# Rows fetched by register on two queues in layers 2 and 3 of a graph network, and the K and V products in halves of the array

## The chip, the cores and the metric

The kernel runs on one core of a Trainium2 chip. The metric is the time of one execution on the device in microseconds. Five engines work side by side on a core: TensorE (PE in the profile), VectorE (DVE), ScalarE (ACT), GpSimd (POOL) and SyncE (SP). SP and ACT can issue transfers between the memory outside the core (DRAM below) and the tiles on the core; GpSimd issues the indirect transfers, which fetch or store one row per lane by a tile of row numbers.

## What is computed

Four layers of a graph network run over 12500 nodes with 64 features each and 400000 edges sorted by destination. After every layer the result is added to the features and normalized:

```python
x = layernorm(x + L0(x))   # max over a node's edges of relu([x_i, x_j - x_i] @ W1 + b1) @ W2 + b2
x = layernorm(x + L1(x))   # edge features summed by source, then a two-layer product
x = layernorm(x + L2(x))   # mean over a node's edges of x[src], a gate of 3 groups, @ W_lin.T + b_lin
x = layernorm(x + L3(x))   # attention: 4 heads, 8 edge types, softmax over a node's edges

# layer 2, the part that matters here
msg_sum = segment_sum(x[src], dst)
# layer 3, the part that matters here
kw, m = typed_head_linear(k[src], rel_att, etype), typed_head_linear(v[src], rel_msg, etype)
a = (kw * qw).sum(-1) * rel_pri[:, etype].T / sqrt(16)
h = segment_sum(m * softmax_by_dst(a), dst)
```

## The kernel before

The edges are laid out as 128 lanes of 3125 edges. Column c of a lane is its c-th edge, and one column over all lanes is a "tile" of 128 edges. Columns are taken in groups of 25 (`G`); there are 124 whole groups, and the last 25 columns are split into groups of 16, 8 and 1 (`groups`). A helper, `gather` (L211), has GpSimd fetch one tile: 128 rows of a table in DRAM, by the 128 numbers in one column.

**The order of the stages.** First the edges are counted and the layer 1 edge features sorted. Then come: the edge stage of layers 0 and 1 (pools `e0`), which writes running results for every edge to the tables R0 and R1; the node stage of both (`n1`), which gathers each node's last row from R0 (tile `ga`) and R1 (tile `g1`), seven 128-node tiles at a time, and writes the features to the table X2; the edge stage of layer 2 (`e2`); its node stage (`n2`), which also makes the tables of layer 3; the edge stage of layer 3 (`e3`); and the last node stage (`n3`).

**Layer 2, edges.** For each group the rows of X2 are fetched into a tile `gx` of 25 columns. VectorE then adds column after column (L1127): what was summed so far, times a 0 or 1 that says whether the edge still belongs to the same node, plus the row. The group then goes to the table R2 in one store on ACT's queue (L1130). In every third group (`ROWS2 = 3`, 41 groups) the last column is not gathered by GpSimd. SP fetches it row by row instead: `row_by_row` loads 16 row numbers (`RL`) into registers (L1112) and issues 16 transfers of 256 bytes (L1117), eight times for a column. There are four `gx` buffers, and the order of the instructions is left to the planner.

**Layer 2, nodes.** For each batch of seven 128-node tiles, `nodes2` gathers the nodes' rows from R2, applies the gate and the product, normalizes, and makes K, V and Q. It then makes, for each of 8 edge types, a row of 128 numbers: 64 of K and 64 of V times that type's matrices. These rows form the table TKM. K lies in partitions 0 to 63 of `kv` and V in 64 to 127; the weights `wkm` hold both products with zeros in between, so that each product of TensorE (L1244) runs over all 128 partitions and yields four edge types. ScalarE moves the result out (L1246). `in_turn` sets the order of these stages by hand for all engines but GpSimd.

**Layer 3, edges.** For each group GpSimd gathers 25 columns of 512-byte rows of TKM into a tile `gk` (three buffers), and SP loads the query rows into `st` (L1273). VectorE carries the queries along the lane (L1278), multiplies and sums for the scores (L1285, L1286), and scans for the running maxima M (L1293). ScalarE takes the exponentials (`weight`, L1301, and `ex`, L1302) and spreads the decays (`dec`, L1308); VectorE forms `wm` (L1313) and runs the scan `hs` (L1318). ScalarE copies hs, M and L into the tile R (L1321 to L1323), and SP stores R to the table R3 (L1324). The planner orders all of it.

Of the kernel before, what the change touches and what calls it, by code (L numbers as in the profile page):

```python
# [9 lines left out]
F32 = mybir.dt.float32  # L10
# [31 lines left out]
WAIT2 = 16  # L42
WAIT3, EVERY3 = 2, 1
ACTN = 3
ROWS2 = 3
RL = 16
ZC = 200


# [1 line left out]
def resnorm_gnn_kernel(ctx: ExitStack, tc: tile.TileContext, a: dict, out: bass.AP):  # L51
# [158 lines left out]
    def gather(to, table, at):  # L210
        return nc.gpsimd.indirect_dma_start(  # L211
            out=to, out_offset=None, in_=table, in_offset=bass.IndirectOffsetOnAxis(ap=at, axis=0)
        )

    def same_keys(psp, sb, key, n, each=None, want_count=False):

# [188 lines left out]
    wkm = const.tile([P, ETY, 2, D], F32, name="wkm")  # L405
    nc.vector.memset(wkm, 0.0)
    for h in range(NH):
        nc.sync.dma_start(
            wkm[D + h * HS : D + (h + 1) * HS, :, 1, h * HS : (h + 1) * HS],
            a["L3_gnn_rel_msg"][h].rearrange("t d o -> d t o"),  # L410
        )

# [408 lines left out]
    with tc.tile_pool(name="ini", bufs=1) as ini, tc.tile_pool(name="inips", bufs=1, space=PSUM) as ips:  # L821
# [31 lines left out]
        for t in range(ETY):  # L853
            pr_ = ips.tile([P, 4, P], F32, name="ps_k")[:D, 0, :D]
            nc.tensor.transpose(pr_, ratt[:, t, :], ident[:D, :D])
            rT = ini.tile([D, D], F32, name="rT", bufs=2)
            nc.vector.tensor_copy(rT, pr_)
            pg = ips.tile([P, 4, P], F32, name="ps_k")[:D, 0, :D]
            nc.tensor.matmul(pg, rT, rT, start=True, stop=True)
            nc.vector.tensor_scalar(wkm[:D, t, 0, :], pg, prib[:, t : t + 1], None, op0=ALU.mult)  # L860


        nothing = ini.tile([1, W3], F32, name="nothing")
# [47 lines left out]
    def ends_of_lanes(sb, table, W, fixG=fixG):  # L911

        row = sb.tile([P, W], F32, name="row", bufs=1)
        gather(row, table[: E + 1, :], fixG)
        return row
# [4 lines left out]
        )  # L920

    to_l0.close()

    with (tc.tile_pool(name="e0", bufs=2) as sb, tc.tile_pool(name="e0ps", bufs=2, space=PSUM) as psp,
          tc.tile_pool(name="e0p1", bufs=1, space=PSUM) as ps1):
# [80 lines left out]
        for g, (c0, ng) in enumerate(groups):  # L1006
            gb = sb.tile([P, ng, D], F32, name="gb", bufs=3)
            if g in early:
                nc.sync.dma_start(gb, early_rows(early[g]))
            else:  # L1010
                for j in range(ng):
                    gather(gb[:, j, :], TB, srcS[:, c0 + j : c0 + j + 1])
            st = sb.tile([P, ng, D], F32, name="st", bufs=3)
            load = nc.sync.dma_start(st, lanes(S)[:, c0 : c0 + ng, :])
            for put in puts0:
                after(load, put, "reads what they write")
            for j in range(ng):
                c = c0 + j
                nc.vector.scalar_tensor_tensor(st[:, j, :], pa, keep[:, c : c + 1], st[:, j, :],  # L1019
                                               op0=ALU.mult, op1=ALU.add)  # L1020
                pa = st[:, j, :]
            R = sb.tile([P, ng, D], F32, name="R", bufs=2)
            for q in range(0, ng, 8):
                n = min(8, ng - q)
                msg = messages(gb, st, q, n, g in early)
                for j in range(q, q + n):
                    c = c0 + j
                    nc.vector.scalar_tensor_tensor(R[:, j, :], pm, negm[:, c : c + 1], msg[:, j - q, :],  # L1028
                                                   op0=ALU.add, op1=ALU.max)
                    pm = R[:, j, :]  # L1030
            nc.sync.dma_start(lanes(R0)[:, c0 : c0 + ng, :], R)
            while done < NG and done * R1G <= g * NG:
                key, pm1 = sums(done, key, pm1)
                done += 1
                if done == NG:
                    end_sums()
        row = ends_of_lanes(sb, R0, D)
        ps = carry_over(ps1, sb, pm)
        u = sb.tile([D, P], F32, name="u0", bufs=1)
        nc.vector.tensor_tensor_scan(u, neg64, ps, NEG, ALU.add, ALU.max)  # L1040
        nc.vector.tensor_max(row, row, shifted(ps1, sb, u, "g0"))
        put_ends(R0, row)


    with tc.tile_pool(name="n1", bufs=1) as sb, tc.tile_pool(name="n1ps", bufs=2, space=PSUM) as psp:
# [5 lines left out]
        def nodes01(b, t0, nt):  # L1051
# [8 lines left out]
            g1 = tile_of([P, nt, D + 1], "g1")  # L1060
            for j in range(nt):
                gather(g1[:, j, :], R1[: E + 1, :], lastE1[:, t0 + j : t0 + j + 1])
            comb = tile_of([P, nt, 2 * D], "comb", 8)
            for _ in range(WAIT1):
                yield
# [24 lines left out]
            nc.sync.dma_start(rows_of(X2, t0, nt), xb)  # L1090

        in_turn(nodes01, [NB] * (NBA - 1) + [4, 2, 1], lambda n: EVERY1)


    with tc.tile_pool(name="e2", bufs=2) as sb, tc.tile_pool(name="e2ps", bufs=1, space=PSUM) as psp:
        pm = sb.tile([P, D], F32, name="m2", bufs=1)
        nc.vector.memset(pm, 0.0)

        single = [g for g in range(2, NG - 1) if g % ROWS2 == 0]
        ns = len(single)  # L1100
        assert single == list(range(single[0], NG - 1, ROWS2)) and ns <= P
        at = groups[single[0]][0] + G - 1
        sf = sb.tile([P, ns], F32, name="sf", bufs=1)
        nc.vector.tensor_copy(sf, srcS[:, at : at + (ns - 1) * ROWS2 * G + 1 : ROWS2 * G])
        ps = psp.tile([P, P], F32, name="ps_i")
        nc.tensor.transpose(ps[:ns, :], sf, ident)
        numbers = sb.tile([P, P], I32, name="numbers", bufs=1)
        nc.vector.tensor_copy(numbers[:ns, :], ps[:ns, :])

        def row_by_row(to, k):  # L1110
            for p in range(0, P, RL):
                _, rows = nc.values_load_multi_w_load_instructions(  # L1112
                    numbers[k : k + 1, p : p + RL], engines=[mybir.EngineType.SP], min_val=0, max_val=NP - 1,
                    skip_runtime_bounds_check_because="src is the number of a node",
                )
                for r, row in enumerate(rows):
                    nc.sync.dma_start(to[p + r : p + r + 1, :], X2[ds(row, 1), :])  # L1117

        for g, (c0, ng) in enumerate(groups):
            gx = sb.tile([P, ng, D], F32, name="gx", bufs=4)  # L1120
            if g in single:
                row_by_row(gx[:, ng - 1, :], single.index(g))
            for j in range(ng - (g in single)):
                gather(gx[:, j, :], X2, srcS[:, c0 + j : c0 + j + 1])
            for j in range(ng):
                c = c0 + j
                nc.vector.scalar_tensor_tensor(gx[:, j, :], pm, keep[:, c : c + 1], gx[:, j, :],  # L1127
                                               op0=ALU.mult, op1=ALU.add)
                pm = gx[:, j, :]
            nc.scalar.dma_start(lanes(R2)[:, c0 : c0 + ng, :], gx)  # L1130
# [34 lines left out]
    with tc.tile_pool(name="n2", bufs=1) as sb, tc.tile_pool(name="n2ps", bufs=2, space=PSUM) as psp:  # L1165
        puts = []

        def nodes2(b, t0, nt):
# [65 lines left out]
            for j in range(nt):  # L1234
# [13 lines left out]
                nc.sync.dma_start(  # L1248
                    TKM[r * ETY : (r + P) * ETY, :].rearrange("(p e) f -> p (e f)", e=ETY),
                    km.rearrange("p w f -> p (w f)"),  # L1250
                )
                yield

# [4 lines left out]
    with tc.tile_pool(name="e3", bufs=2) as sb, tc.tile_pool(name="e3ps", bufs=1, space=PSUM) as psp:  # L1258
# [9 lines left out]
        for c0, ng in groups:  # L1268
            gk = sb.tile([P, ng, 2 * D], F32, name="gk", bufs=3)
            for j in range(ng):  # L1270
                gather(gk[:, j, :], TKM, stS[:, c0 + j : c0 + j + 1])
            st = sb.tile([P, ng, D], F32, name="st", bufs=2)
            load = nc.sync.dma_start(st, lanes(S)[:, c0 : c0 + ng, :])  # L1273
            for put in puts:
                after(load, put, "reads what they write")
            for j in range(ng):
                c = c0 + j
                nc.vector.scalar_tensor_tensor(st[:, j, :], pa, keep[:, c : c + 1], st[:, j, :],  # L1278
# [44 lines left out]
            nc.scalar.activation(R[:, :, D + NH :], L.rearrange("p h c -> p c h"), AF.Copy)  # L1323
# [117 lines left out]
```

## Time and profile before

| What | Value |
|---|---|
| Time, median of 3 runs | 16696.17 us (16695.95 to 16697.46) |
| Time of the profiled execution | 16699.22 us |
| Its span, first to last instruction | 16697.4 us |
| Busy: POOL, DVE, PE, ACT | 12548.5, 9601.6, 5362.8, 2673.4 us |
| Mean granted TensorE clock | 0.628 |
| Gathers of layer 2 (gx), of layer 3 (gk) | 3084, 3125 |
| Rows fetched by SP in layer 2 | 5248 |

A busy share is an average over stages that have different limits. In the list of groups a line gives the source line, the engine, the operation, what is written and read, the count, then busy time, mean length in nanoseconds and the idle time before these instructions with what ended it. "issue" is time in which the engine waited for nothing that the profile shows. SPq and ACTq are the instructions on those engines that issue transfers or work on registers; they are not counted as busy.

### The profile page before, as it was taken

How to read it: one execution, taken by the hardware profiler on the slowest of the kernel's cores; microseconds unless marked ns; L12 is line 12 of the kernel's file. 1: busy time of each engine (PE TensorE's matmuls, PEld its weight loads, DVE VectorE, ACT ScalarE, POOL GpSimd, SP SyncE). 2: the span in 40 equal slices, each digit the busy share in tenths (PEclk: the TensorE clock that was granted, in tenths of full speed). 3: DMA queues.
4: the chain of work that ended last, by engine and by line, in shares of the span. 5: the costliest groups of instructions: out<-in, count | busy, mean ns of one | idle time of the engine just before them, and what ended most of it. 6: DMA issues, size and time to landing. Idle time of an engine off the chain costs nothing. (4 is left out here: it accounts for less than half of the span.)

```text
span 16697.4 us, 162726 instructions
## 1 busy us (share of the span) xinstructions
PE 5362.8 (32%) x42392; PEld 4426.1 (27%) x42392; DVE 9601.6 (58%) x28242; ACT 2673.4 (16%) x4960; POOL 12548.5 (75%) x13066
## 2 busy tenths in 40 slices
PE   4445666666653666666400000000051000000002
PEld 4444555554542555555300000000030000000002
DVE  9996777777753777776322222222235565555556
ACT  0012333333321111111100000000022122122112
POOL 7777777777777777777777777777776777777776
PEclk6667777777766777777655555555575555555555
DMA  2333333222222555555211111111143333333333
GB/s 81 119 103 90 85 85 85 63 54 54 53 53 57 203 199 198 205 200 172 60 52 52 55 53 55 53 55 53 54 146 128 107 109 109 107 108 107 109 107 97
DMA packets 1116080, 1640.30 MB, mean 98 GB/s; under 512 B 740851, under 2 KB 741235, under 8 KB 1114755
## 3 DMA queue, kind: packets, MB, share of 16 engines
q1 hardware_dynamic: 653490, 987.85, 17.6%
q0 software_dynamic: 417824, 533.15, 12.2%
q10 hardware_dynamic: 43824, 108.83, 1.7%
q8 instruction: 337, 5.52, 0.1%
q14 instruction: 605, 4.95, 0.1%
HBM read 891.71 MB, written 737.15 MB: 98 GB/s over the span
## 5 line engine op out<-in xcount | busy, mean ns | idle before, releaser
L734 POOL DMA_INDIRECT SRT<-at,to x3125 | 3036.9, 972 | 952.5 <-issue 945.5
L211 POOL DMA_INDIRECT gk<-TKM,stS x3125 | 2975.6, 952 | 952.4 <-issue 926.8
L211 POOL DMA_INDIRECT gx<-X,srcS x3084 | 2921.0, 947 | 966.9 <-issue 907.5
L1127 DVE SCALAR_TENSOR_TENSOR gx<-gx,keep 128x64 f32<-128x64 f32 x3124 | 917.9, 294 | 2945.4 <-DMA gx<-X,srcS 1839.7
L211 POOL DMA_INDIRECT gb<-TB,srcS x2125 | 2076.0, 977 | 651.7 <-issue 625.2
L1028 DVE SCALAR_TENSOR_TENSOR R<-R,negm,msg 128x64 f32<-128x64 f32 x3124 | 854.0, 273 | 791.3 <-PE msg L959 786.9
L899 PE MATMUL ps_c<-ident,full 128*64 128x128 f32 x3 | 1.3, 421 | 3943.1 <-DVE full L1330 3942.0
L899 PE MATMUL ps_c<-ident,gx 128*64 128x128 f32 x1 | 0.4, 422 | 3867.6 <-DVE gx L1127 3867.6
L1285 DVE TENSOR_TENSOR pr<-st,gk 128x320 f32<-128x320 f32 x627 | 308.3, 492 | 1556.5 <-DMA gk<-TKM,stS 1551.5
L211 POOL DMA_INDIRECT xg<-in_x,srcS x1000 | 954.9, 955 | 306.0 <-issue 299.6
L899 PEld LDWEIGHTS ps_c<-ident,full 128*64 128x64 f32 x3 | 0.4, 129 | 3944.5 <-DVE full L1330 3942.8
L899 PEld LDWEIGHTS ps_c<-ident,gx 128*64 128x64 f32 x1 | 0.1, 129 | 3867.9 <-DVE gx L1127 3867.9
L337 DVE TENSOR_TENSOR ol<-iota,lo 128x512 f16<-128x512 f32 (+2 forms) x1000 | 979.1, 979 | 0.0
L1278 DVE SCALAR_TENSOR_TENSOR st<-st,keep 128x64 f32<-128x64 f32 x3124 | 868.4, 278 | 46.1
L953 PE MATMUL pt<-ident,st 128*128 128x128 f32 (+1 forms) x3250 | 825.9, 354 | 213.8 <-DVE st L1019 196.2
L1019 DVE SCALAR_TENSOR_TENSOR st<-st,keep 128x64 f32<-128x64 f32 x3124 | 863.7, 276 | 1.5
L694 PE MATMUL pG<-ol,mb 128*128 128x128 f16 x4625 | 778.0, 242 | 195.4 <-ACT mb L678 193.9
L987 DVE SCALAR_TENSOR_TENSOR r<-r,keep 128x64 f32<-128x64 f32 x3000 | 830.4, 277 | 0.1
L334 DVE TENSOR_TENSOR oh<-iota,hi 128x392 f16<-128x392 f32 (+2 forms) x1000 | 784.3, 784 | 24.0 <-DMA xg<-in_x,srcS 24.0
L646 PE MATMUL pT<-identh,oh 128*98 128x128 f16 x3125 | 413.3, 263 | 1180.3 <-DVE oh L334 1178.2
L952 PE MATMUL pt<-ident,gb 128*128 128x128 f32 (+1 forms) x2210 | 571.6, 353 | 565.6 <-DMA gb<-TB,srcS 561.3
L694 PE MATMUL pG<-A,hT 98*128 98x128 f16 x3125 | 732.3, 244 | 0.0
(325 smaller groups left out, 18349.9 us busy)
## 6 DMA issues: line engine op xcount, KB each, us to landing
st<-S SPq DMA_DIRECT2D x248, 800.0 KB
R<-R SPq DMA_DIRECT2D x124, 900.0 KB
r<-SRT SPq DMA_DIRECT2D x125, 812.5 KB
R<-r SPq DMA_DIRECT2D x125, 812.5 KB
S<-zero SPq DMA_DIRECT2D x200, 500.0 KB
R<-R SPq DMA_DIRECT2D x124, 800.0 KB
R<-gx ACTq DMA_DIRECT2D x124, 800.0 KB
gx<-X SPq DMA_DIRECT2D x5248, 0.2 KB
```

The lines of the kernel that those rows point to most:

```text
L211: return nc.gpsimd.indirect_dma_start(out=to, out_offset=None, in_=table, in_offset=bass.IndirectOffsetOnAxis(ap=at, axis=0))
L334: nc.vector.tensor_tensor(oh, iota[:, None, :NT].to_broadcast([P, n, NT]), hi[:, :, None].to_broadcast([P, n, NT]), ALU.is_equal)
L337: nc.vector.tensor_tensor(ol, iota[:, None, :].to_broadcast([P, n, P]), lo[:, :, None].to_broadcast([P, n, P]), ALU.is_equal)
L694: nc.tensor.matmul(pG[:, j, :], l, r, start=(n == 0), stop=(n == len(terms) - 1))
L734: put = nc.gpsimd.indirect_dma_start(out=SRT, out_offset=bass.IndirectOffsetOnAxis(ap=to[:, j : j + 1], axis=0), in_=at[:, j, :], in_offse ...
L952: nc.tensor.matmul(pt[:w, k, :], two_tiles(gb, k, w), ident, start=True, stop=False)
L953: nc.tensor.matmul(pt[:w, k, :], two_tiles(st, k, w), ident, start=False, stop=True)
L987: nc.vector.scalar_tensor_tensor(r1[:, j, :D], pm1, keep1[:, c : c + 1], r1[:, j, :D], op0=ALU.mult, op1=ALU.add)
L1019: nc.vector.scalar_tensor_tensor(st[:, j, :], pa, keep[:, c : c + 1], st[:, j, :], op0=ALU.mult, op1=ALU.add)
L1028: nc.vector.scalar_tensor_tensor(R[:, j, :], pm, negm[:, c : c + 1], msg[:, j - q, :], op0=ALU.add, op1=ALU.max)
L1127: nc.vector.scalar_tensor_tensor(gx[:, j, :], pm, keep[:, c : c + 1], gx[:, j, :], op0=ALU.mult, op1=ALU.add)
L1278: nc.vector.scalar_tensor_tensor(st[:, j, :], pa, keep[:, c : c + 1], st[:, j, :], op0=ALU.mult, op1=ALU.add)
```

## The change

There are four parts.

**Layer 2.** Of every five groups two (`g % 5` in 1 and 3, 49 groups) have their last two columns fetched row by row, 98 columns in all. SP fetches the last but one and ACT the last, row for row in turn. The row numbers are first multiplied by the size of a row on VectorE (`places_of`), so that a register holds a byte offset into the table seen as bytes. Registers are loaded 32 at a time. The rows of a group are issued two groups ahead; the store of R2 goes to SP's queue; there are five `gx` buffers; SP and ACT keep the order in which the program is written.

**Layer 3.** Every third group (41 groups) has its last two columns fetched the same way, 82 in all, half of the rows at the end of the step three groups ahead and the other half at the end of the step two ahead. The load of `st` is issued two groups ahead, with three buffers. SP and ACT keep program order here too, and ACT copies hs, M and L in the order of the text.

**K and V products.** `wkm` loses its zeros: K uses partitions 0 to 63 and V 64 to 127, one product of 512 columns each, both issued before the two copies.

**Node stage of layers 0 and 1.** The gathers of R1 for the first 28 node tiles are issued at the end of the edge stage, around the repair of R0's lane ends.

```diff
-ROWS2 = 3
-RL = 16
+ROWS2 = 5, (1, 3)
+ROWS3 = 3
+RL = 32
...
+    def places_of(psp, sb, columns, size, name):
+        n = columns.shape[1]
+        f = sb.tile([P, n], F32, name=f"{name}_f", bufs=1)
+        nc.vector.tensor_copy(f, columns)
+        ps = psp.tile([P, P], F32, name="ps_i", bufs=1)
+        nc.tensor.transpose(ps[:n, :], f, ident)
+        t = sb.tile([n, P], I32, name=name, bufs=1)
+        nc.vector.tensor_scalar(t, ps[:n, :], float(size), None, op0=ALU.mult)
+        return t
+
+    def row_by_row(table, size, p, *parts):
+        rows = [
+            nc.values_load_multi_w_load_instructions(
+                places[:, p : p + RL], engines=[kind], min_val=0, max_val=table.shape[0] - size,
...
+            )[1]
+            for engine, kind, to, places in parts
+        ]
+        for r in range(RL):
+            for (engine, kind, to, places), at in zip(parts, rows):
+                engine.dma_start(to[p + r : p + r + 1, :].bitcast(mybir.dt.uint8), table[None, ds(at[r], size)])
...
+        def sums_early(n):
+            for t in range(n):
+                t += first_sums[0]
+                gather(g1s[:, t, :], R1[: E + 1, :], lastE1[:, t : t + 1])
+            first_sums[0] += n
+
+        sums_early(NS - 8)
         row = ends_of_lanes(sb, R0, D)
+        sums_early(5)
...
         put_ends(R0, row)
+        sums_early(3)
...
+        with tc.manual_schedule(engines={SP, ACT}):
+            for g, (c0, ng) in enumerate(groups):
+                if g + 2 in single:
+                    to, k = tiles_of(g + 2), 2 * single.index(g + 2)
+                    for p in range(0, P, RL):
+                        row_by_row(X2b, 4 * D, p, (nc.sync, SP, to[:, G - 2, :], places[k : k + 1, :]),
+                                   (nc.scalar, ACT, to[:, G - 1, :], places[k + 1 : k + 2, :]))
+                gx = tiles_of(g)
+                for j in range(ng - 2 * (g in single)):
+                    gather(gx[:, j, :], X2, srcS[:, c0 + j : c0 + j + 1])
...
+                nc.sync.dma_start(lanes(R2)[:, c0 : c0 + ng, :], gx)
...
-                km = sb.tile([P, 2, ETY * D], F32, name=f"km_{j % 4}")
-                for w in range(2):
-                    pw = psp.tile([P, ETY * D], F32, name="pw", bufs=4)
-                    nc.tensor.matmul(pw, kv[:, s], wkm[:, w * ETY // 2 : (w + 1) * ETY // 2].rearrange("p e s f -> p (e s f)"),
+                km = sb.tile([P, ETY, 2, D], F32, name=f"km_{j % 4}")
+                pws = [psp.tile([P, ETY, D], F32, name="pw", bufs=4) for _ in range(2)]
+                for w, pw in enumerate(pws):
+                    of = slice(w * D, (w + 1) * D)
+                    nc.tensor.matmul(pw.rearrange("p e f -> p (e f)"), kv[of, s], wkm[of].rearrange("p e f -> p (e f)"),
                                      start=True, stop=True)
-                    nc.scalar.activation(km[:, w, :], pw, AF.Copy)
+                for w, pw in enumerate(pws):
+                    nc.scalar.activation(km[:, :, w, :], pw, AF.Copy)
...
+        def step(g, c0, ng):
...
             nc.sync.dma_start(lanes(R3)[:, c0 : c0 + ng, :], R)
             last = ng
+            del gks[g]
+            if g + 2 < len(groups):
+                load_starts(g + 2)
+            for ahead, half in ((3, 0), (2, 1)):
+                if g + ahead in single3:
+                    to, k = keys_of(g + ahead), 2 * single3.index(g + ahead)
+                    for p in range(half * P // 2, (half + 1) * P // 2, RL):
+                        row_by_row(TKMb, 8 * D, p, (nc.sync, SP, to[:, G - 2, :], places3[k : k + 1, :]),
+                                   (nc.scalar, ACT, to[:, G - 1, :], places3[k + 1 : k + 2, :]))
+
+        R = None
+        with tc.manual_schedule(engines={SP, ACT}):
+            load_starts(0)
+            load_starts(1)
+            for g, (c0, ng) in enumerate(groups):
+                step(g, c0, ng)
```

More of the change, by code (lines that the diff above doesn't have):

```diff
@@ L213, in gather, with bytes_of @@
         )
+    def bytes_of(table):
+        return table.rearrange("n f -> (n f)").bitcast(mybir.dt.uint8)
+    def places_of(psp, sb, columns, size, name):
[11 more added lines that the diff above has]
+                places[:, p : p + RL], engines=[kind], min_val=0, max_val=table.shape[0] - size,
+                skip_runtime_bounds_check_because="these are numbers of nodes, or of nodes and edge types",
+            )[1]
[4 more added lines that the diff above has]
+                engine.dma_start(to[p + r : p + r + 1, :].bitcast(mybir.dt.uint8), table[None, ds(at[r], size)])
+    SP, ACT = mybir.EngineType.SP, mybir.EngineType.Activation
     def same_keys(psp, sb, key, n, each=None, want_count=False):
@@ L403, in resnorm_gnn_kernel @@
     nc.sync.dma_start(wa, a["L3_gnn_Wa"].rearrange("(h t) i o -> (t i) h o", t=2))
-    wkm = const.tile([P, ETY, 2, D], F32, name="wkm")
+    wkm = const.tile([P, ETY, D], F32, name="wkm")
     nc.vector.memset(wkm, 0.0)
@@ L408, in resnorm_gnn_kernel @@
         nc.sync.dma_start(
-            wkm[D + h * HS : D + (h + 1) * HS, :, 1, h * HS : (h + 1) * HS],
+            wkm[D + h * HS : D + (h + 1) * HS, :, h * HS : (h + 1) * HS],
             a["L3_gnn_rel_msg"][h].rearrange("t d o -> d t o"),
@@ L859, in resnorm_gnn_kernel @@
             nc.tensor.matmul(pg, rT, rT, start=True, stop=True)
-            nc.vector.tensor_scalar(wkm[:D, t, 0, :], pg, prib[:, t : t + 1], None, op0=ALU.mult)
+            nc.vector.tensor_scalar(wkm[:D, t, :], pg, prib[:, t : t + 1], None, op0=ALU.mult)
         nothing = ini.tile([1, W3], F32, name="nothing")
@@ L922, in resnorm_gnn_kernel @@
     to_l0.close()
+    NS = 4 * NB
+    to_n1 = ExitStack()
+    g1s = to_n1.enter_context(tc.tile_pool(name="g1s", bufs=1, side=right)).tile([P, NS, D + 1], F32, name="g1s")
+    first_sums = [0]
     with (tc.tile_pool(name="e0", bufs=2) as sb, tc.tile_pool(name="e0ps", bufs=2, space=PSUM) as psp,
@@ L1059, in nodes01 @@
                 gather(ga[:, j, :], R0[: E + 1, :], lastE[:, t0 + j : t0 + j + 1])
-            g1 = tile_of([P, nt, D + 1], "g1")
-            for j in range(nt):
-                gather(g1[:, j, :], R1[: E + 1, :], lastE1[:, t0 + j : t0 + j + 1])
+            if t0 + nt <= NS:
+                g1 = g1s[:, cols, :]
+            else:
+                g1 = tile_of([P, nt, D + 1], "g1")
+                for j in range(nt):
+                    gather(g1[:, j, :], R1[: E + 1, :], lastE1[:, t0 + j : t0 + j + 1])
             comb = tile_of([P, nt, 2 * D], "comb", 8)
@@ L1092, in resnorm_gnn_kernel @@
         in_turn(nodes01, [NB] * (NBA - 1) + [4, 2, 1], lambda n: EVERY1)
+    to_n1.close()
     with tc.tile_pool(name="e2", bufs=2) as sb, tc.tile_pool(name="e2ps", bufs=1, space=PSUM) as psp:
@@ L1097, in resnorm_gnn_kernel @@
         nc.vector.memset(pm, 0.0)
[L1099 to L1130, printed above, removed]
+        single = [g for g in range(2, NG - 1) if g % ROWS2[0] in ROWS2[1]]
@@ new lines, in resnorm_gnn_kernel @@
+        assert 2 * len(single) <= P
+        cols = sb.tile([P, len(single), 2], I32, name="cols", bufs=1)
+        for k, g in enumerate(single):
+            at = groups[g][0] + G - 2
+            nc.vector.tensor_copy(cols[:, k, :], srcS[:, at : at + 2])
+        places = places_of(psp, sb, cols.rearrange("p k t -> p (k t)"), 4 * D, "places")
+        single3 = list(range(3, NG - 1, ROWS3))
+        assert 2 * len(single3) <= P
+        cols3 = sb.tile([P, len(single3), 2], I32, name="cols3", bufs=1)
@@ new lines, in resnorm_gnn_kernel, with tiles_of @@
+        for k, g in enumerate(single3):
+            at = groups[g][0] + G - 2
+            nc.vector.tensor_copy(cols3[:, k, :], stS[:, at : at + 2])
+        places3 = places_of(psp, const, cols3.rearrange("p k t -> p (k t)"), 8 * D, "places3")
+        X2b = bytes_of(X2)
+        gxs = {}
+        def tiles_of(g):
+            if g not in gxs:
+                gxs[g] = sb.tile([P, groups[g][1], D], F32, name="gx", bufs=5)
+            return gxs[g]
+        with tc.manual_schedule(engines={SP, ACT}):
[8 more added lines that the diff above has]
+                    gather(gx[:, j, :], X2, srcS[:, c0 + j : c0 + j + 1])
+                for j in range(ng):
+                    c = c0 + j
+                    nc.vector.scalar_tensor_tensor(gx[:, j, :], pm, keep[:, c : c + 1], gx[:, j, :],
+                                                   op0=ALU.mult, op1=ALU.add)
+                    pm = gx[:, j, :]
+                nc.sync.dma_start(lanes(R2)[:, c0 : c0 + ng, :], gx)
+                del gxs[g]
@@ L1249, in nodes2 @@
                     TKM[r * ETY : (r + P) * ETY, :].rearrange("(p e) f -> p (e f)", e=ETY),
-                    km.rearrange("p w f -> p (w f)"),
+                    km.rearrange("p e w f -> p (e w f)"),
                 )
@@ L1267, in resnorm_gnn_kernel, with keys_of, load_starts @@
         last = G
[L1268 to L1273, printed above, removed]
+        TKMb = bytes_of(TKM)
+        gks, sts = {}, {}
+        def keys_of(g):
+            if g not in gks:
+                gks[g] = sb.tile([P, groups[g][1], 2 * D], F32, name="gk", bufs=3)
+            return gks[g]
+        def load_starts(g):
+            c0, ng = groups[g]
+            sts[g] = sb.tile([P, ng, D], F32, name="st", bufs=3)
+            load = nc.sync.dma_start(sts[g], lanes(S)[:, c0 : c0 + ng, :])
             for put in puts:
                 after(load, put, "reads what they write")
+        def step(g, c0, ng):
+            nonlocal pa, M, L, hs, last, R
+            gk, st = keys_of(g), sts.pop(g)
+            for j in range(ng - 2 * (g in single3)):
+                gather(gk[:, j, :], TKM, stS[:, c0 + j : c0 + j + 1])
             for j in range(ng):
```

## The prediction, made before the change was run

> **What bounds the kernel now.** I read the page first, then the groups by line, then each stage that the change touches: windows by stage, the lines of the row fetch on SyncE (SP), its queue's waits, and the timeline of one group.
>
> ```profile
> span 16697.4 us, 162726 instructions
> ...
> ACT  0012333333321111111100000000022122122112
> POOL 7777777777777777777777777777776777777776
> ...
> L211 POOL DMA_INDIRECT gk<-TKM,stS x3125 | 2975.6, 952 | 952.4 <-issue 926.8
> L211 POOL DMA_INDIRECT gx<-X,srcS x3084 | 2921.0, 947 | 966.9 <-issue 907.5
> ```
>
> GpSimd is at 7 tenths from end to end, and the idle time before its gathers is "issue", about 0.3 us each: nothing holds it up. A gather costs its place in that line. In layer 2 the 3084 gathers run from 8417.1 to 12278.2 us, 1.252 us each; in layer 3 the 3125 run from 12602.1 to 16529.8, 1.257 each, so three groups of 25 take 94.3 us. A gather taken off GpSimd saves that much, as long as nothing else becomes slower than GpSimd. ScalarE (ACT) is near 0 in layer 2 and at 2 in layer 3.
>
> ```profile
> L1117 SPq FUSED_REGOPS  x5248: 37/37/52, 8417.2 to 12273.2; - x195
> L1117 SPq MOVE gx<-X x5248: 29/29/38, 8417.8 to 12273.3; - x195
> L1117 SPq DMA_DIRECT2D gx<-X x5248: 224/225/955, 8417.9 to 12273.3; - x195
> ...
> L1112 SPq TENSOR_LOAD <-numbers x328: 1134/1252/1662, 8415.9 to 12265.7; - x164
> ...
> L474 SPq TENSOR_LOAD <-flag x1: 511/511/511, 45.2 to 45.2; - x1
> ...
> SPq L1117 <- DMA R<-gx: 1204.2, 102, 32.9
> ```
>
> This is the price of a row now. Start to start a row takes 0.408 us: 0.073 from FUSED_REGOPS (the multiplication of the row number) to MOVE, 0.060 to the DMA, 0.275 to the next row. Eight loads of 16 registers add 1.30 us each, so a tile of 128 rows holds SP 63 us. The last line is a wait of another sort: rows wait for the stores of R2. The trace's semaphore events show why: SP's and ACT's transfers share one round of eight semaphores, and each transfer waits for the one eight places before it to land, whichever queue issued it.
>
> ```profile
> 14050.03 0.38 ACT L1322 ACTIVATE R<-M 128x100 f32<-128x100 f32 x1 [19.69 <-DVE M L1293]
> ...
> 14050.56 0.26 ACT L1301 ACTIVATE weight<-ex 128x100 f32<-128x100 f32 x1
> ...
> 14051.25 1.56 ACT L1308 ACTIVATE dec<-ex 128x1664 f32<-128x1664 f32 x1
> ...
> 14052.75 0.35 ACT L1323 ACTIVATE R<-L 128x100 f32<-128x100 f32 x1
> ...
> 14054.67 3.61 DVE L1318 TENSOR_TENSOR_SCAN hs<-dec,wm 128x1664 f32<-128x1664 f32 x1
> ...
> 14058.31 3.23 ACT L1321 ACTIVATE R<-hs 128x1600 f32<-128x1600 f32 x1 [5.21 <-DVE hs L1318]
> ```
>
> One group of layer 3, by start and length. ACT is idle for most of the 31.4 us, but it sits twice in a serial chain: `weight` and `dec` go to VectorE (DVE), whose scan `hs` ends 7.7 us after `weight` began, and R<-hs ends 11.0 us after it. What is queued on ACT between R and the next group's `weight` delays that group.
>
> ```profile
> 12378.70:12399.30 20.60, 20.60 (x85) 12.01 (x85) 8.53 (x19) 11.74 (x22) 15.79 (x16) 1.00 0.68 238
> ...
> 8116.55 0.94 POOL L211 DMA_INDIRECT gb<-TB,srcS  x1 [0.30 <-PE pt L953]
> 8133.76 0.94 POOL L211 DMA_INDIRECT row<-R,fixG  x1 [16.27 <-DMA R<-R]
> 8136.96 0.99 POOL L918 DMA_INDIRECT R<-row,fixS  x1 [2.25 <-DVE row L1041]
> 8139.95 0.97 POOL L211 DMA_INDIRECT ga<-R,lastE  x1 [2.00 <-DMA R<-row,fixS]
> ```
>
> The window is one batch of the node stage after layer 2 (columns: time, PE, weight load, DVE, ACT, POOL): TensorE is busy for all of it. The timeline shows the one hole of GpSimd, 22.4 us between layer 0's edges and its nodes.
>
> **Layer 2.** GpSimd loses 98 − 41 = 57 gathers: 57 × 1.252 = −71 us. SP and ACT now fetch two tiles in each of 49 groups of 125. Byte offsets replace the multiplication, so I take a row as 0.408 − 0.073 = 0.335 us. No row shows ACT issuing rows; its large store takes 326 ns to issue where SP's take 319 to 373, so I price ACT like SP. But the alternation gives each queue four of the eight semaphores: a row waits until its queue's row four places back has landed. The events put a landing 1.23 us after issue (median), a quarter above 1.37, a tenth above 1.56. The recorded landings, put in order through that rule, give 0.39 us per row (0.34 with eight). Ends: 0.28 (the MOVE gone too and little waiting) and 0.50 (landings near 2 us, or two queues that hinder each other). A load of 32 registers: one value took 0.51 us and 16 took 1.25, so 0.05 each and 2.0 for 32. A tile is then 128 × 0.39 + 4 × 2.1 = 58 us. The stores of R2 move from ACT's queue to SP's, behind the rows: five groups give SP 2 × 58 + 5 × 0.4 = 118 us of work in 3 × 31.3 + 2 × 28.8 = 151.5 us of GpSimd. The rows go out two groups ahead, a store is late by one batch of rows, and with five buffers nobody needs its tile by then. So GpSimd still sets the pace, up to about 0.52 us a row. The some 90 small copies for `cols` (0.16 us each, the nearest row is a 128x4 copy, 15 us) cost nothing: DVE is busy 919 of 3869 us here.
>
> **Layer 3.** If GpSimd still set the pace, 82 gathers would go, −103 us, and three groups would take 91.8. I do not think it does. Of every three steps, two end with 64 rows on SP and 64 on ACT, and both queues now keep program order, so the next `weight` stands behind ACT's rows. From one `weight` (0): R<-hs to 11.0, then R<-M and R<-L, 11.7. SP issues the store of R3 and the load of st for two groups on, at 11.8 and 12.2. Alone these land after 3.7 and 4.3 us; together I take the load as landed at 17.5. ACT loads 32 registers (to 13.8), issues three rows, and the fourth comes to the semaphore that the st load holds: wait to 17.5. Then 61 rows × 0.39 = 23.8, the second load 2.1, one gap of instruction fetch 0.3: the next `weight` at 43.7. The third step has no rows: 7.7 us to the end of `hs`, then DVE's rest of the next group, 13.4 us where nothing of it is done before, 6 where the st recurrence is; I take 9, so 17. Three groups: 2 × 43.7 + 17 = 104 us against 94.3, and over 41 such triples +9.7 × 41 = +398 us. The row price moves this by 61 × 2 × 41 = 5.0 us per nanosecond: 0.28 would put `weight` at 37 and leave GpSimd as the bound (−103), 0.50 gives 50.4 and +970.
>
> Two rules stand against these rows. The Trainium skill, "DMA: Bandwidth & Descriptors", section "Issuing engines are not separate DMA queues", says that issuing from several engines saves only sequencer time, usually small beside the transfer. Here the row's packet takes 15 to 18 ns and its issue 335: for rows the issue is the whole price. By the rule ACT's rows would be near free and layer 3 would give −103; by the rows +398. I go by the rows. The same page, "Latency and other measured facts", has a `tensor_load` floor of about 600 ns. At that price, an estimate, for 32 registers `weight` would come about 2.9 us sooner (two loads), three groups take 98 and layer 3 cost +160; the trace's 1.25 us for 16 says that it grows with the count, so I stay at 2.0.
>
> **Node stage after layer 0.** 28 gathers of R1 (1.27 us each, 35.6) leave it. Twenty go into the hole and run 25.1 us from 8117.5, so the row gather comes at 8142.7 instead of 8133.8 (+8.9); five stand in a wait of 2.25 (+4.1), three in one of 2.00 (+1.8). Net −35.6 + 14.8 = −21. If they landed among gathers elsewhere it would be 0.
>
> **Node stage after layer 2.** The pw products take 28 passes of 0.43 us, 12.1 of a batch's 20.6. The same number of matmuls is issued, each with 64 rows. No row shows two halves at once; the skill's "TensorEngine Tiling (Array Packing)", "Theoretical Speedup", gives up to 2x. By that estimate TensorE needs 14.6 and GpSimd's 14 operations of 1.27 are next, 17.8: −2.8 to −5 a batch, at most −45. If the halves run one after the other: 0. I take −25. The evictions on ACT (196 of 0.6 us) stay.
>
> **Sum.** −71 + 398 − 21 − 25 = +281. The profiled execution took 16699.2 us, 1.8 outside its span, and 3 above the median of 16696.2; from the median: 16977 us.
>
> **Rivals.** (1) Likeliest, 0.55: ACT's rows bound layer 3, three groups in 98 to 113 us: 16740 to 17350. (2) GpSimd keeps layer 3, 0.25: rows at 0.28 us or the rows' semaphores never late, `weight` at 37.5 or sooner. Then −103 − 71 − 21 − 25 = −220, 16476. For it: ACT is busy only 20% there. Against: the chain is serial, and the 0.335 already drops the multiplication. It decides from three groups in 97.1 us, where layer 3's loss equals the other 117 us of gain. (3) Rows at 0.50, 0.12: +970 − 117, 17550; SP then nearly bounds layer 2 too. (4) Between, 0.08: 95 to 98 us per three groups, 16615 to 16740. The halves not running together is +25 in any case. This kernel's measurement tells about 0.2%, 33 us, from no change. Faster 0.29, same 0.04, slower 0.67; the range from 16450 takes in (2) and goes to 17380, beyond (1).
>
> **What would show it.** In the profile after: groups of gk gathers spaced unevenly and three of them in about 104 us, with POOL idle before gk and waiting for DVE's wm; ACT's `weight` 35 us or more after R in two steps of three; ACT and SP rows 0.39 us apart, with no FUSED_REGOPS; register loads of 2 us; gx gathers still 1.25 us apart. POOL at 7 in layer 3 with gk still 1.26 us apart would make the prediction wrong, and so would a row below 0.29 us; gx gathers with long waits would make layer 2 wrong.

## The result: slower by 4.3%, and the profile after

The changed kernel takes 17412.92 us (median of 4 runs, 17408.53 to 17416.31) against 16696.06 for the kernel before: a ratio of 1.0429, 95% interval 1.0411 to 1.0447. The forecast was +281 us; it is +717, just outside the range. The granted clock is 0.621 against 0.628 in the two profiled executions, and TensorE is not at work in the stage that lost the time.

The stages, from the first to the last gather of each kind, in the two profiled executions:

| Stretch | Before | After | Difference | Forecast |
|---|---|---|---|---|
| start to the first gx gather | 8417.1 | 8409.7 | -7.4 | -21 |
| gx gathers, layer 2 | 3860.2 | 3782.8 | -77.4 | -71 |
| last gx to first gk (node stage 2) | 324.9 | 294.1 | -30.8 | -25 |
| gk gathers, layer 3 | 3926.7 | 4737.5 | +810.8 | +398 |
| last gk to the end | 168.6 | 187.1 | +18.5 | none |
| span | 16697.4 | 17411.4 | +714.0 | +281 |

First the page after: the span, ACT's and GpSimd's 40 slices, and the two gather groups (busy time, mean ns of one | idle time before them, and what ended most of it).

```profile
span 17411.4 us, 192228 instructions
...
ACT  0013333333221111111100000000311111111112
POOL 7777777777777777777777777777666666666665
...
L212 POOL DMA_INDIRECT gk<-TKM,stS x3043 | 2898.2, 952 | 1840.5 <-issue 892.4
...
L212 POOL DMA_INDIRECT gx<-X,srcS x3027 | 2860.3, 945 | 951.0 <-issue 890.2
```

A gather costs what it did, 0.95 us. In layer 2 its idle time is still "issue", 0.3 us a gather. In layer 3 GpSimd has fallen from 7 tenths to 6: 1840.5 us of idle time where 952.4 stood before, and only 892.4 of it is "issue". ACT's busy digit fell from 2 to 1 although ACT became the bound: issuing rows is not counted as busy. What the rest of the idle time waited for is in the list of waits (us in total, times, longest):

```profile
ACT weight L1372 <- DMA gk<-TKM: 2584.9, 80, 34.4
...
DVE wm L1384 <- ACT weight L1372: 596.3, 81, 15.0
POOL gk L212 <- DVE wm L1384: 570.0, 40, 15.6
...
DVE st L1349 <- DMA st<-S: 441.6, 95, 8.2
...
POOL gk L212 <- DVE ex L1368: 328.1, 41, 8.5
```

Read from the bottom up this is the chain of the forecast. GpSimd waits for a `gk` buffer, which `wm` frees; `wm` waits for `weight`; `weight` stands 80 times, two in each of some 40 triples of groups, for about 32 us behind ACT's own rows.

The rows themselves, by the trace's view of their line (min/median/max ns):

```profile
L243 ACTq MOVE gk<-TKM x5248: 29/29/29, 12533.5 to 17208.3; - x195
L243 ACTq DMA_DIRECT2D gk<-TKM x5248: 234/234/1037, 12533.5 to 17208.4; - x195
L243 SPq MOVE gk<-TKM x5248: 29/29/29, 12540.6 to 17211.6; - x195
L243 SPq DMA_DIRECT2D gk<-TKM x5248: 227/228/400, 12540.6 to 17211.6; - x195
```

FUSED_REGOPS is gone. Start to start, a row of layer 3 takes 0.351 us on either queue as a median, and as a mean 0.397 on ACT and 0.408 on SP (the forecast said 0.39). Here and below waits of over 2 us between two rows are left out of a row's price. ACT has two of them in each step with rows, early in it, of 3.4 us as a mean: one for the store of R3 and one for the load of `st`. A load of 32 registers takes 2.25 us as a median (forecast 2.0).

Then one triple of steps on ACT, start and length:

```profile
14020.83 0.26 ACT L1372 ACTIVATE weight<-ex 128x100 f32<-128x100 f32 x1 [32.09 <-DMA gk<-TKM]
...
14028.56 3.22 ACT L1392 ACTIVATE R<-hs 128x1600 f32<-128x1600 f32 x1 [5.22 <-DVE hs L1389]
...
14032.21 0.24 ACT L1372 ACTIVATE weight<-ex 128x100 f32<-128x100 f32 x1
...
14039.92 3.24 ACT L1392 ACTIVATE R<-hs 128x1600 f32<-128x1600 f32 x1 [5.23 <-DVE hs L1389]
14042.58 0.47 ACTq L243 DMA_DIRECT2D gk<-TKM  x1
...
14043.48 32.76 ACTq L243 DMA_DIRECT2D gk<-TKM  x62
14076.29 0.26 ACT L1372 ACTIVATE weight<-ex 128x100 f32<-128x100 f32 x1 [32.60 <-DMA gk<-TKM]
...
14098.92 3.20 ACT L1392 ACTIVATE R<-hs 128x1600 f32<-128x1600 f32 x1 [20.13 <-DVE hs L1389]
...
14102.50 22.66 ACTq L243 DMA_DIRECT2D gk<-TKM  x34
```

The step without rows goes from `weight` to `weight` in 11.4 us. The next takes 44.1: 64 rows stand in ACT's order between the large copy R<-hs and `weight`, 62 of them in the last 32.8 us. The step after it should look the same, but here R<-hs starts 22.6 us after `weight`, not 8: VectorE was late with `hs`. This is VectorE in that step:

```profile
14064.55 0.48 DVE L1356 TENSOR_TENSOR pr<-st,gk 128x320 f32<-128x320 f32 x1
...
14070.46 0.49 DVE L1356 TENSOR_TENSOR pr<-st,gk 128x320 f32<-128x320 f32 x1 [4.91 <-DMA gk<-TKM,stS]
...
14076.86 0.49 DVE L1356 TENSOR_TENSOR pr<-st,gk 128x320 f32<-128x320 f32 x1 [5.39 <-DMA gk<-TKM,stS]
...
14089.13 0.49 DVE L1356 TENSOR_TENSOR pr<-st,gk 128x320 f32<-128x320 f32 x1 [5.19 <-DMA gk<-TKM,stS]
...
14091.50 0.81 DVE L1384 TENSOR_TENSOR wm<-gk,weight 128x400 f32<-128x400 f32 x1
```

`weight` is there at 14076.29, and `wm` needs nothing else; yet it starts at 14091.50. VectorE's order is the planner's, and that order puts the next group's products `pr` ahead of this group's `wm`. They wait for gathers that come one by one at GpSimd's pace, late because GpSimd had itself waited 15 us for a buffer ahead of this run of gathers:

```profile
14025.07 0.94 POOL L212 DMA_INDIRECT gk<-TKM,stS  x1 [15.04 <-DVE wm L1384]
```

The forecast had the wait of `wm` nowhere.

Over groups 6 to 117 of layer 3 the means in us, from one `weight` to the next, by the place of the step in its triple:

| Kernel | first row step | second row step | step without rows | three groups | layer 3, gk gathers |
|---|---|---|---|---|---|
| before | 31.4 | 31.4 | 31.4 | 94.3 | 3926.7 |
| forecast | 43.7 | 43.7 | 17 | 104 | 4325 |
| after | 44.4 | 58.1 | 11.4 | 113.8 | 4737.5 |

### The profile page after: what moved, and what is told of

Same layout as the page of the kernel before. It is cut to its first block, busy times and chain, and to the rows that moved or that the text cites. A ratio compares the mean times of both kernels' runs of the same rounds, so it can differ in the third digit from the quotient of the medians.

```text
span 17411.4 us, 192228 instructions
## 1 busy us (share of the span) xinstructions
PE 5324.1 (31%) x42393; PEld 4411.1 (25%) x42393; DVE 9776.4 (56%) x28334; ACT 2636.0 (15%) x4960; POOL 12405.0 (71%) x12927
## 5 line engine op out<-in xcount | busy, mean ns | idle before, releaser
L212 POOL DMA_INDIRECT gk<-TKM,stS x3043 | 2898.2, 952 | 1840.5 <-issue 892.4
L212 POOL DMA_INDIRECT gx<-X,srcS x3027 | 2860.3, 945 | 951.0 <-issue 890.2
L1349 DVE SCALAR_TENSOR_TENSOR st<-st,keep 128x64 f32<-128x64 f32 x3124 | 887.9, 284 | 540.1 <-DMA st<-S 441.6
```

Of the source, the lines that this page charges most:

```text
L212: return nc.gpsimd.indirect_dma_start(out=to, out_offset=None, in_=table, in_offset=bass.IndirectOffsetOnAxis(ap=at, axis=0))
```

## The experiments

The theory: ACT's rows in program order ahead of `weight` are the loss in layer 3, and VectorE's order adds to it. The rivals: the rows of SP do the harm (the store of R3 and the load of `st` stand behind them); or program order on SP and ACT does it, rows or not; or the row price rules all. The kernels below are the changed kernel with the edits shown. Each result stands beside the kernel before on the same chip. Some runs were on chips on which the kernel before itself takes 24.3 to 24.6 ms; they have a paragraph of their own at the end.

**Layer 3 as before.** The edge loop of layer 3 of the kernel before, with all other parts of the change.

```diff
+        for c0, ng in groups:
+            gk = sb.tile([P, ng, 2 * D], F32, name="gk", bufs=3)
+            for j in range(ng):
+                gather(gk[:, j, :], TKM, stS[:, c0 + j : c0 + j + 1])
+            st = sb.tile([P, ng, D], F32, name="st", bufs=2)
...
-        with tc.manual_schedule(engines={SP, ACT}):
-            load_starts(0)
-            load_starts(1)
-            for g, (c0, ng) in enumerate(groups):
-                step(g, c0, ng)
```

> The run with layer 3's edge stage of before, once more, since in the first four runs the kernel before itself took 24302 us. If this chip runs the kernel before in about 16696 us: theory (the whole loss is in layer 3): 16581 us, gk gathers 1.257 us apart, 3928 us for the stage. Rival (the other three parts bring part of the loss): over 16660.

16597.59 us against 16695.21 (0.994, interval 0.9918 to 0.9963). Layer 3 is back at 3927.1 us. So the three other parts together gain 98 us (forecast 117), and all of the loss, 815 us, lies in layer 3 and what follows it.

**Only ACT fetches rows in layer 3**, the last column of the 41 groups; GpSimd gathers the last but one.

```diff
-            for j in range(ng - 2 * (g in single3)):
+            for j in range(ng - (g in single3)):
...
-                        row_by_row(TKMb, 8 * D, p, (nc.sync, SP, to[:, G - 2, :], places3[k : k + 1, :]),
-                                   (nc.scalar, ACT, to[:, G - 1, :], places3[k + 1 : k + 2, :]))
+                        row_by_row(TKMb, 8 * D, p, (nc.scalar, ACT, to[:, G - 1, :], places3[k + 1 : k + 2, :]))
```

> ScalarE's rows alone, once more. Theory (ScalarE's rows and VectorE's order bound layer 3): weight to weight near 44 and 58 us in the two steps with rows, the whole 17230 to 17410. Rival (the two queues hold each other up): 16530 to 16700.

17307.03 us (1.0367, 1.0337 to 1.0397); layer 3 takes 4632.1. With SP's rows gone a row on ACT takes 0.345 us as a mean, not 0.397, its median 0.333: alone, it waits less for the semaphore eight places back, which is what the forecast read from the events of before. The first row step falls to 40.3 us, but the second is as long as in the changed kernel (59.3), so SP's rows are not what makes it long.

**Only SP fetches rows in layer 3.** The same edit with SP in the place of ACT: the same 41 columns are fetched by row, and ACT issues none.

```diff
+                        row_by_row(TKMb, 8 * D, p, (nc.sync, SP, to[:, G - 1, :], places3[k + 1 : k + 2, :]))
```

> SyncE's rows alone in layer 3, once more for such a chip. Theory (ScalarE's rows bound layer 3): GpSimd keeps the pace, layer 3 3876 us, the whole 16546. Rival (late rows or SyncE's program order hold up VectorE too): layer 3 over 3980 us, the whole over 16650.

16547.05 us against 16698.83 (0.9909, 0.988 to 0.9938), one microsecond from its forecast, which is partly luck: layer 3 is 7 us shorter than forecast, and the tail after the last gather takes 185.2 us, 16 more than with layer 3 as before. Layer 3 takes 3869.4, and its page has GpSimd at 7 tenths with "issue" alone before the gathers:

```profile
POOL 7777777777777777777777777777777777777776
...
L212 POOL DMA_INDIRECT gk<-TKM,stS x3084 | 2930.4, 950 | 940.2 <-issue 925.2
```

The pair decides it. 5248 rows cost +760 us against this kernel when ACT issues them, and gain 50 against layer 3 as before when SP does. Program order on SP and ACT is the same in both, so it is not the cause without ACT's rows; nor are the loads of `st` behind SP's rows. One more order can be ruled out here. GpSimd's is the planner's too, and it fetches what is left to gather of a group with rows ahead of the two groups before it: in the changed kernel runs of 23 and of 50 gathers alternate between GpSimd's waits. The kernel with SP's rows has this order as well, its steps are 41.4, 31.3 and 20.2 us, and no gather of layer 3 there waits longer than 0.32 us.

**VectorE in program order too**, all else as in the changed kernel: `wm` comes ahead of the next group's products.

```diff
-        with tc.manual_schedule(engines={SP, ACT}):
+        with tc.manual_schedule(engines={SP, ACT, mybir.EngineType.DVE}):
             load_starts(0)
```

> VectorE in program order in layer 3, once more for a chip that runs the kernel before in 16696 us. Theory (planned order puts the next group's products ahead of wm): weight to the end of hs 7.7 us in all three steps, steps of about 44, 44 and 22 us, 111 against 113.8; the whole near 17300. Rival (late gathers hold VectorE in any order): hs over 15 us after weight in the second step, the whole 17410 or more.

17267.83 us (1.0341, 1.0311 to 1.0371), 145 us less than the changed kernel. The three steps are 44.7, 43.4 and 22.2 us, and `hs` ends 8.1 us after `weight` in each. On ACT:

```profile
14022.91 0.26 ACT L1372 ACTIVATE weight<-ex 128x100 f32<-128x100 f32 x1 [32.82 <-DMA gk<-TKM]
...
14065.73 0.26 ACT L1372 ACTIVATE weight<-ex 128x100 f32<-128x100 f32 x1 [30.92 <-DMA gk<-TKM]
...
14087.95 0.26 ACT L1372 ACTIVATE weight<-ex 128x100 f32<-128x100 f32 x1 [10.34 <-DVE ex L1369]
```

The second row step is now as long as the first, as the forecast had it: the 14.6 us between 58.1 and 43.4 were VectorE's order. But the step without rows grows from 11.4 to 22.2. While VectorE waited in the changed kernel it had done the next group's products; in program order all of them come after `hs`: 22.2 - 8.1 = 14.1 us. Most of the planner's delay is given back one step later, and only 3.5 of the 14.6 us are net (113.8 against 110.3).

**The recurrence of the next group ahead of `weight`.** As the last one, and in row steps VectorE also carries the queries of the next group along the lane (25 operations, 8 us) while it waits for ACT.

```diff
+            if g % 3 and g + 1 < len(groups):
+                carry(g + 1)
             weight = psp.tile([P, NH, ng], F32, name="weight", bufs=2)
```

> The query recurrence ahead of wm, once more for such a chip. Theory: steps of 44, 44 and 14 us, 102 in place of 110; the whole near 16930. Rival (the gathers or the load of st are next in line): 108 or more, the whole over 17200.

16953.01 us (1.0154, 1.0124 to 1.0183); the steps are 44.4, 43.8 and 14.3 us, three groups 102.6. The step without rows fell by 8 us, to 8.1 + 6.2. This is close to the forecast's own picture, three groups in 104 us, and the time is 24 us from the forecast of 16977: a kernel that does nearly what the forecast supposed takes nearly the time that it gave. Part of the nearness is luck: layer 3 costs 57 us less than forecast, and the tail and the node stage of layers 0 and 1 give 38 us of that back.

**A quarter of the rows in every step.** One group in four has its two last columns fetched by row, 32 rows per queue in each step, with four `gk` buffers: 60 columns instead of 82.

```diff
-ROWS3 = 3
+ROWS3 = 4
...
-            for ahead, half in ((3, 0), (2, 1)):
+            for ahead, half in ((4, 0), (3, 1), (2, 2), (1, 3)):
...
-                    for p in range(half * P // 2, (half + 1) * P // 2, RL):
+                    for p in range(half * P // 4, (half + 1) * P // 4, RL):
```

> The quarters once more, for a chip that runs the kernel before in 16696 us. Theory (the next weight comes 28.5 to 29 us after the last, under GpSimd's 31): layer 3 3852 us, the whole 16522. Rival (ScalarE's rows in the chain cost more than they save): layer 3 over 3930 us, the whole over 16600.

16681.21 us against 16696.54 (0.9991, 0.9981 to 1.0001): no clear gain, where 16522 was expected. Steps take 32.2 us each, 0.7 more than before, and layer 3 3987.7. ACT's rows fit within GpSimd's time here, so something else was late. The list of waits shows VectorE at the load of `st`:

```profile
DVE st L1349 <- DMA st<-S: 1044.8, 120, 12.4
```

The changed kernel had 441.6 us of this wait. The planner's order has the recurrence of the group after next, whose load was issued only a step ago, before the products of the next group.

**The same with VectorE in program order.** The `quarters` edit and the `manual_schedule` edit together.

> The quarters (32 rows a step on each queue, 60 columns of layer 3), with VectorE in program order too. Theory (in the quarters of before it was again VectorE's planned order, which put the query recurrence of the group after next, waiting for the load of st, ahead of the next group's products): weight to weight 31 us, GpSimd keeps the pace, layer 3 3852 us, the whole 16522. Rival (the rows of ScalarE themselves, with the stores' semaphores, take over 31 us a step): layer 3 stays near 3988 us, the whole near 16680.

16550.54 us against 16705.55 (0.9909, 0.988 to 0.9937). The steps are 31.0 us as a mean, three groups 93.0, and GpSimd has its pace again:

```profile
L212 POOL DMA_INDIRECT gk<-TKM,stS x3065 | 2927.6, 955 | 934.8 <-issue 887.9
```

The time is 28 us over the expected 16522: layer 3 takes 3861.2 us, 9 more, and the tail 190.0, 21 more than with layer 3 as before. In the list of waits:

```profile
ACT weight L1372 <- DMA gk<-TKM: 1522.9, 88, 19.7
```

`weight` still waits for ACT's rows, 17 us at a time. VectorE still waits for ACT (600.1 us for `ex`, which ACT makes right behind `weight`), but no gather waits longer than 0.32 us any more, so these waits cost nothing. So the planner's order of VectorE was the 131 us of the last run, with the same rows on ACT. Rows on ACT are no loss in themselves; with 64 of them in one step the stage loses, in program order on VectorE too (17267.83 us, above).

**SP alone, in every second group**: 60 columns, as many as in the quarters, with four buffers and VectorE in program order.

```diff
-ROWS3 = 3
+ROWS3 = 2
...
-            for ahead, half in ((3, 0), (2, 1)):
+            for ahead, half in ((4, 0), (3, 1)):
```

> SyncE alone in layer 3, the last column of every second group (60 columns), 64 rows a step, four gk buffers, VectorE in program order. Theory: SyncE needs 64 x 0.334 + 2 x 2.3 = 26 us a step and some 4 for the stores' semaphores, under GpSimd's 31: layer 3 3852 us, the whole 16522. Rival (SyncE is late with the load of st, which stands behind its rows): layer 3 over 3930 us, the whole over 16600.

16568.59 us (0.9919, 0.9891 to 0.9948). With 19 gathers fewer than the kernel with 41 SP columns, layer 3 takes 3866.4 us, only 3.0 less, where 19 x 1.25 = 24 were due: the gathers stand 1.262 us apart, not 1.255, and the tail after the last one is 193.7 us, not 185.2. It is the gather itself that takes longer, 957 ns in place of 950; the idle time between two is the same. Why was not settled. No kernel tried here with more rows than SP's 41 columns was faster.

**On the other chips.** Layer 3 as before, SP alone, ACT alone, VectorE in program order, quarters and the carried recurrence also ran on three chips where the kernel before takes 24302 to 24562 us. Their ratios there:

| Kernel | Ratio, where before takes 24.3 to 24.6 ms | Ratio, where it takes 16.7 ms |
|---|---|---|
| layer 3 as before | 1.0098 | 0.994 |
| quarters (two chips) | 1.038, 1.0377 | 0.9991 |
| SP rows only (two chips) | 1.0572, 1.0563 | 0.9909 |
| ACT rows only | 1.0572 | 1.0367 |
| recurrence carried | 1.0684 | 1.0154 |
| VectorE in program order (two chips) | 1.0716, 1.072 | 1.0341 |

With layer 3 as before, nine in ten of SP's rows follow within 2.80 us there, and three in four within 1.41; on the other chip it is 0.58 and 0.37. Layer 2 then takes 6472 us instead of 3791, and GpSimd waits for it (the gather's group, then the list of waits):

```profile
L212 POOL DMA_INDIRECT gx<-X,srcS x3027 | 2872.5, 949 | 3628.6 <-DVE gx L1175 2525.0
```

```profile
DVE gx L1175 <- DMA gx<-X: 4769.8, 49, 101.4
```

This is the forecast's rival of dear rows, seen in layer 2: its estimate was that from about 0.52 us a row the queue bounds the stage. It says nothing about the chip of the result. What makes rows dear on those chips was not settled. Expected of the first four of these runs:

> Layer 3's edge stage is that of the kernel before, the other three parts of the change stay. Theory (the whole loss is in layer 3, where ScalarE's rows and VectorE's order hold up the chain; the other parts gain what the traces show: layer 2 -77, the nodes after it -27, the nodes of layers 0 and 1 about -11): 16581 us, gk gathers 1.257 us apart, 3928 us for the stage. Rival (part of the loss comes from the other parts, for example layer 2's rows): over 16660.

> Layer 3 keeps the new order and SyncE's rows (128 in two of three steps, the last column), GpSimd gathers the other column, ScalarE issues no rows. Theory (ScalarE's rows bound layer 3): GpSimd keeps the pace, 41 gathers fewer than before: layer 3 takes 3876 us and the whole 16530. Rival (rows landing late, or SyncE's program order, hold up VectorE): layer 3 stays well over 4000 us, the whole over 16700.

> The mirror of it: ScalarE issues its 64 rows in two of three steps, GpSimd gathers SyncE's column. Theory: weight to weight stays near 44 and 58 us in the two steps with rows, a little less since the rows now have all eight semaphores (0.33 in place of 0.36 us a row, 2 us a step): layer 3 4550 to 4740 us, the whole 17230 to 17410. Rival (the two queues hold each other up): most of the loss goes, the whole near 16530 to 16700.

> As after, but VectorE too keeps program order in layer 3, so that no product of the next group stands before wm of this one. Theory (in the second step of three hs ends 22.6 us after weight and not 7.7, because VectorE's planned order puts the next group's products, which wait for GpSimd's gathers, ahead of wm): weight to hs is 7.7 us in all three steps, the steps take 44, 44 and about 22 us: 111 against 113.8, the whole near 17300. Rival (the late gathers hold VectorE in any order): hs still ends over 15 us after weight in the second step.

## Why the prediction went wrong in size

**The side and the mechanism held.** The chain is that of the likeliest case: ACT's rows ahead of `weight`, then `wm`, the buffer, GpSimd. The first row step was put at 43.7 us and took 44.4. The pair of ACT and SP alone shows it. The parts of the 43.7 held too: in the triple above the wait for the load of `st` ended 18.2 us after `weight` (put at 17.5), and the rows behind it took 25.9 (put at 26.2).

**Layer 2** was put at -71 and gave -77. Rows take 0.324 us (SP) and 0.334 (ACT) as medians, 0.38 and 0.42 as means, and GpSimd keeps its 1.25 us a gather. By the rule that the forecast set against itself (the Trainium skill, "DMA: Bandwidth & Descriptors", section "Issuing engines are not separate DMA queues": the sequencer time of an issue is usually small beside the transfer), ACT's rows in layer 3 would have been near free; the 760 us between ACT alone and SP alone show that it does not hold for these rows.

**The second row step: the term that failed first.** The working took "7.7 us to the end of `hs`" from the trace of before and used it in every step. In before VectorE waits for gathers as well, but there its order has `wm` right behind `weight` (14050.56), and the next group's products only behind `hs`:

```profile
14050.88 0.81 DVE L1313 TENSOR_TENSOR wm<-gk,weight 128x400 f32<-128x400 f32 x1
...
14058.38 0.48 DVE L1285 TENSOR_TENSOR pr<-st,gk 128x320 f32<-128x320 f32 x1
```

For the changed kernel the planner made another order, with the next group's five products ahead of `wm` in one step of three. Since their rows are late, `hs` ends 22.6 us after `weight` there, in place of 7.7. The forecast named both queues' new program order, and did not ask what VectorE's order would be.

**The step without rows: the term that failed second.** It was put at 17 us, with 9 for "DVE's rest of the next group", between 13.4 and 6. Program order measured 14.1, the carried recurrence 6.2: both ends were about right, and the choice between them was a guess. In the changed kernel itself the rest was done early, in the wait of the step before, and the step took 11.4, so this miss is hidden in the 58.1.

**How the 436 us of the miss come together.** In the changed kernel's own steps, times 41 triples: the second row step adds 590 us (58.1 in place of 43.7), the first 29 (44.4), and the step without rows gives 230 back (11.4 in place of 17). Another 16 are the forecast's own rounding: 2 x 43.7 + 17 is 104.4, and the working counted 104 (its +160 for the cheaper register load has the same rounding and would be 176). That is 405 of the 413 that layer 3 missed by.

The kernel with VectorE in program order splits it by cause. It takes 145 us less: that is what the planner's order costs net. Of what is left there, the rows are 41 x (44.7 + 43.4 - 87.4) = 29 us, the step without rows 41 x (22.2 - 17) = 213, and the rounding 16. The tail is 23 us longer than before, the node stage of layers 0 and 1 is 14 over its forecast; layer 2 and its nodes, 11 better than forecast, go the other way. Together these are 429 of 436.

**Node stage after layer 0.** -21 was forecast, -7.4 came. The forecast put twenty gathers of R1 into the hole of 16.3 us ahead of the row gather. The timeline shows the hole still there:

```profile
8145.19 0.94 POOL L212 DMA_INDIRECT gb<-TB,srcS  x1 [0.30 <-PE pt L989]
8162.47 0.94 POOL L212 DMA_INDIRECT row<-R,fixG  x1 [16.34 <-DMA R<-R]
8165.65 0.99 POOL L950 DMA_INDIRECT R<-row,fixS  x1 [2.24 <-DVE row L1085]
```

GpSimd isn't among the engines whose order is set by hand, and all 28 gathers stand earlier, between 7892 and 8021 us, among the gathers of the edge stage. There they cost their full place in the line, so the nodes begin 28.9 us later and then take 36 us less. This is the end "if they landed among gathers elsewhere" of the forecast, or near it.

**Node stage after layer 2.** -25 was forecast, -30.8 came. The forecast's own bounds do not fit each other: 14 batches at -2.8 to -5 us are -39 to -70, not at most -45, so the -25 was a guess that came close. The same stage is 29 to 32 us shorter in every kernel of the experiments on such chips. The groups of TensorE's `pw` before and after (busy us, mean ns):

```profile
L1244 PE MATMUL pw<-wkm,kv 128*128 128x512 f32 x392 | 175.7, 599 | 0.0
```

```profile
L1301 PE MATMUL pw<-wkm,kv 64*128 64x512 f32 x392 | 118.9, 635 | 10.8 <-ACT km L1304 10.8
```

As many products, each no shorter, and together busy for 57 us less: the two halves overlap, in part, by a factor of 1.5 where the estimate took 2. The stage gains only 31 of these 57. ACT's copies, 0.60 us each as before, now hold TensorE's weight loads up (48.8 us of waits; in before they wait at most 1.2 us for copies); that these are what eats the rest was not tested.

## What to carry to other kernels

Cost a row fetch by the engine that issues it, not by the transfer: here 64 rows were some 32 us in which nothing else in that engine's program started, so rows belong on an engine that has nothing in the chain of the stage. An order that a planner chose holds only while its inputs come in time; when a change makes one input late, ask of every engine that keeps such an order what stands ahead of the next link of the chain. Here the simplest version is as good as any: the change with only SP's rows in layer 3 takes 16547 us, 152 less than before and 866 less than the change as made; the quarters with VectorE in program order, 16551, are not told apart from it.

## What the runs showed of the hardware

- SP's and ACT's rows slow each other through their eight shared semaphores: a row on ACT takes 0.345 us as a mean with ACT alone in layer 3, and 0.397 with both. With both, 82% of ACT's rows there that come 0.37 to 2 us behind the last start within 25 ns of the landing of the transfer that held their semaphore; with ACT alone none does.
- A load of 32 registers takes 2.25 us, where 16 took 1.25 and one 0.51. Rows pay 0.07 us each for it, about a fifth of their price.
- ACT's row transfers begin before its own copies end: in the triple above the first row goes out at 14042.58, while R<-hs runs to 14043.16. The copies of M and L are interleaved with the rows, although the program has them first.
- The same kernel can take 24.5 ms on one chip and 16.6 on another, and rows by register suffer from it far more than gathers do: in layer 2 SP's rows went from a 90th percentile of 0.58 us to 2.80, while a gather stayed at 949 ns.
